# A two-layer graph network on one core: the activations' transposes move from TensorE to VectorE and DMA, with another order of tokens

## The chip, the core and the metric

The kernel runs on one core of one Trainium2 chip. The metric is the device time of one launch in microseconds, the median of several runs; smaller is better. Besides the timed runs there is one profiled execution, whose trace gives the start and length of each instruction on each engine. The engines are TensorE (PE, with its weight loads as PEld), VectorE (DVE), ScalarE (ACT), GpSimd (POOL) and SyncE (SP), which here issues every DMA.

## What is computed

The input `x` holds 64 graphs of 256 tokens with 512 features in float32, and `adj` is one 256 x 256 adjacency matrix for all of them. Each of two layers normalizes the tokens, applies a relu and adds its result to `x`:

```python
h = relu(layernorm(x));  x = x + (adj @ h) @ W0 + b0            # layer 0
h = relu(layernorm(x))                                          # layer 1, 8 heads of 64
q, k, v = h @ Wq + bq, h @ Wk + bk, h @ Wv + bv
s = q @ k.T / 8 + (1 - adj) * -1e9
x = x + (softmax(s) @ v) @ Wo + bo
```

All of it stays in float32. Layer 0 and the attention treat all tokens alike, so the tokens of a graph may be held in any order, as long as `adj` and the output are read and written in the same order.

## The kernel before

Two graphs make a group of 512 tokens, and 32 groups follow one another. In SBUF a tile has 128 partitions. `x` of a group is held by token, as four slices of 128 tokens with 512 features each (slices 0 and 1 are the first graph, k=0; slices 2 and 3 the second, k=1).

Five weight products (layer 0's `w`, then `q`, `k`, `v` and `o`) run through `project` (line 397), which computes a product of 2 x 2 blocks with seven block products in place of eight. For that GpSimd prepares sums of blocks of the activations, `t1` to `t4` (class `Halves`, lines 370 to 387), named `t_y`, `t_h` and `t_o` for the three inputs. One block product is 8 records on TensorE. In the order of `project` these are a11, a12, s2, s1, s3, a22, s4; the third (s2) is added on top of the first in the same PSUM bank, so it must wait until the first one's result has been read out, and it needs the sum t2.

The order of the work is written out by hand. The loop over groups (lines 706 to 726) puts these pieces after one another on TensorE: attention of group g, first half (`attend`, `pav` and `pden`); scores of its second half (`score`, line 608); output product of the group before (`post`, `o`); queries and keys of the next group (`queries_keys`); attention of the second half; scores of the next group; its values (`values`, `v`); and layer 0 of the group after next (`layer0`, `py` and `w`). Each engine works in program order. `after` and `tick` put work of the other engines a stated number of steps later. In each group TensorE needs 87 us for this round.

The step that changes stands at the start of `queries_keys`. The weight products want the activations with features on partitions. At the end of `layer0`, `finish` (line 500) adds and measures the result on VectorE, GpSimd computes the scales (`norm_scales`, lines 53 and 54), and ScalarE writes the normalized `h1` by token (line 512), k=0 first and then k=1. Later, `queries_keys` transposes `h1` into `h1T` with 16 TensorE transposes against an identity (line 525, tile `ph`, four PSUM banks), which ScalarE and VectorE copy out in turn (lines 527 and 529). GpSimd then forms `t_h` from `h1T` (line 387).

Three more places matter for the working. In `score`, VectorE reads each of eight score banks (line 613), and GpSimd subtracts the largest mask value (line 616). In `attend`, VectorE inverts the denominators in four pieces (line 656) and divides two tiles (line 660), which `post` uses as its input; GpSimd's `t_o` is formed directly behind the second division (lines 663 to 670). At the start, `adj` is transposed once on TensorE (line 318), and the masks are made from that copy (lines 328 to 339).

Eight PSUM banks are handed out in order by `bank` and `give`. `h1T` shares one buffer with layer 0's `yT` (tag "bT"), and the sums t1 to t4 rotate through eight buffers, two sets.

Of the kernel before, what the change touches and what calls it, by code (L numbers as in the profile page):

```python
# [13 lines left out]
P = 128  # L14
# [184 lines left out]
def kernel(  # L199
# [52 lines left out]
    def give(t):  # L252
        free_banks.append(bank_of.pop(id(t))[0])

    clock, later = [0], []

    def after(delay, fn, *args):
        later.append((clock[0] + delay, len(later), fn, args))  # L260

    def tick():
        clock[0] += 1
        due = sorted(e[:2] for e in later if e[0] <= clock[0])
        run_now = [e for d in due for e in later if e[:2] == d]
        later[:] = [e for e in later if e[0] > clock[0]]
        for _, _, fn, args in run_now:
            fn(*args)

    X, H0, Q, K, V, OT, HO = {}, {}, {}, {}, {}, {}, {}  # L270

    def load(g):
        X[g] = xpool.tile([P, T, D], F32, tag="x", name=f"x_{g}")
        src = x[g * GB:(g + 1) * GB].rearrange("b (t p) d -> p (b t) d", p=P)
        for t in range(0, T, 1 if g == 0 else T):
            e = t + (1 if g == 0 else T)
            nc.sync.dma_start(X[g][:, t:e, :], src[:, t:e, :])

    def quarter(xt, i, k):

# [1 line left out]


    load(0)
    adj_sb = tmp.tile([P, NT, N], F32, tag="u", name="adj_sb")
    nc.sync.dma_start(adj_sb, adj.rearrange("(t p) m -> p t m", p=P))
    w0_sb = load_weight(nc, const, w0, "w0_sb")
# [24 lines left out]


    adjT = const.tile([P, NT, N], F32, name="adjT")
    pa = bank([P, NT, N], "pa")
    for k in range(NT):
        for t in range(NT):
            nc.tensor.transpose(pa[:, k, t * P:(t + 1) * P], adj_sb[:, t, k * P:(k + 1) * P], ident)
    nc.vector.tensor_copy(adjT, pa)
    give(pa)  # L320

# [3 lines left out]
    top_b = top[:, None, :].to_broadcast([P, 2 * NT, N])  # L325

    def masks():
        nc.vector.tensor_scalar(maskT, adjT, -1.0, 1.0, op0=ALU.mult, op1=ALU.add)
        nc.vector.tensor_scalar(maskT, maskT, MASKED, None, op0=ALU.mult)
        nc.vector.tensor_scalar(adj_sb, adj_sb, -1.0, 1.0, op0=ALU.mult, op1=ALU.add)  # L330
        nc.vector.tensor_scalar(adj_sb, adj_sb, MASKED, None, op0=ALU.mult)
        rowmax = small.tile([P, NT], F32, tag="rowmax", name="rowmax", bufs=1)
        nc.vector.tensor_reduce(rowmax, adj_sb, AX.X, ALU.max)
        spread = tmp.tile([P, NT, P], F32, tag="u", name="spread")
        nc.vector.tensor_copy(spread, rowmax[:, :, None].to_broadcast([P, NT, P]))
        pt = bank([P, N], "pt")
        for t in range(NT):
            nc.tensor.transpose(pt[:, t * P:(t + 1) * P], spread[:, t, :], ident)
        nc.vector.tensor_copy(top, pt)
        give(pt)  # L340
# [15 lines left out]

    def weight_sums(eng, w, name):
        def part(i, j):  # L360
            return w[:, 2 * j:2 * j + 2, i * HF:(i + 1) * HF]
        s = {n: const.tile([P, 2, HF], F32, name=f"{name}_{n}") for n in ("s1", "s2", "s4")}
        eng.tensor_tensor(s["s1"], part(1, 0), part(1, 1), op=ALU.add)
        eng.tensor_tensor(s["s2"], s["s1"], part(0, 0), op=ALU.subtract)
        eng.tensor_tensor(part(1, 0), part(0, 0), part(1, 0), op=ALU.subtract)
        eng.tensor_tensor(s["s4"], part(0, 1), s["s2"], op=ALU.subtract)
        s.update(a11=part(0, 0), a12=part(0, 1), a22=part(1, 1), s3=part(1, 0))
        return s

    class Halves:  # L370

        def __init__(self, name, chunks):
            self.chunks = chunks
            self.t = {n: act.tile([P, 2, N], F32, tag="t", name=f"{n}_{name}", bufs=8)
                      for n in ("t1", "t2", "t3", "t4")}

        def b(self, j, k, c):
# [11 lines left out]
    def product(ps, s, a, halves, b, by_token, start=True, stop=True):  # L389
        for m in range(2):  # L390
            for c in range(2):
                w, y = s[a][:, c, :], halves.operand(b, c)
                lhs, rhs = (y, w) if by_token else (w, y)
                nc.tensor.matmul(ps[:, m, :], lhs[:, m * P:(m + 1) * P], rhs, start=(start and m + c == 0), stop=(c == 1),  # L394
                                 skip_group_check=True)

    def project(s, halves, by_token, name, read, finish, first_half_first=False):
# [67 lines left out]
        for t in range(T):  # L465
            after(start + T + 3 + t, relu, t)

    H1, H1T = {}, {}

    def layer0(g):  # L470

# [18 lines left out]

        mv = small.tile([P, T, 2], F32, tag="mv", name=f"mv1_{g}")
        st = [small.tile([P, 2, nc.vector.BN_STATS_DIM], F32, tag="st1", name=f"st1_{g}_{t}", bufs=8) for t in range(T)]
        h1 = H1[g] = act.tile([P, T, D], F32, tag="h", name=f"h1_{g}")
        done = []

        def read(ps, n):
# [15 lines left out]
                    nc.scalar.activation(h1[:, k * NT + t, :], xt[:, k * NT + t, :], AF.Relu,  # L512
                                         bias=nb[:, t:t + 1], scale=rs[:, t:t + 1])

        yield from project(W0, halves, True, f"w_{g}", read, finish)

    def queries_keys(g):

        xt, h1 = X[g], H1.pop(g)
        h1T = act.tile([P, DC, GN], F32, tag="bT", name=f"h1T_{g}")  # L520
        halves = H1T[g] = Halves(f"h_{g}", [h1T[:, d, :] for d in range(DC)])
        for t in range(T):
            ps = bank([P, DC, P], f"ph_{g}_{t}")
            for d in range(DC):
                nc.tensor.transpose(ps[:, d, :], h1[:, t, d * P:(d + 1) * P], ident)  # L525
            if t % 2:
                nc.vector.tensor_copy(h1T[:, :, t * P:(t + 1) * P], ps)  # L527
            else:
                nc.scalar.copy(h1T[:, :, t * P:(t + 1) * P], ps)
            give(ps)  # L530
        for c in range(2):
            halves.sums(nc.gpsimd, c, ("t1", "t2"))
        for c in range(2):
            halves.sums(nc.gpsimd, c, ("t3", "t4"))
        yield

        def out_bias_add(t):
            nc.gpsimd.tensor_tensor(xt[:, t, :], xt[:, t, :], bo_r, op=ALU.add)  # L538

        for s, bias, store, n in ((WQ, bq_c, Q, "q"), (WK, bk_c, K, "k")):  # L540
            store[g] = {}

            def read(ps, m):
                if m == 4:
                    return
                u = partial(f"{n}_{g}", m)
                for c in range(2):
                    f = 2 * (m == 3) + c
                    nc.scalar.activation(u[:, c, :], ps[:, c, :], AF.Identity, bias=bias[:, f:f + 1])
                return u  # L550

            def finish(ps, u, i, k):
                o = store[g][i, k] = act.tile([P, 2, N], F32, tag=f"{n}{i}{k}", name=f"{n}_{g}_{i}{k}")
                add(o, ps, u)

            if n == "k":
                for t in range(T):
                    after(2 * t + 1, out_bias_add, t)
            yield from project(s, halves, False, f"{n}_{g}", read, finish)

    def values(g):
        halves = H1T.pop(g)
# [10 lines left out]
            o = V[g][i, k] = act.tile([P, NT, HF], F32, tag=f"v{i}{k}", name=f"v_{g}_{i}{k}")  # L573
            add(o, ps, u)

        yield from project(WV, halves, True, f"v_{g}", read, finish)

    def post(g):

# [8 lines left out]
        def finish(ps, u, i, k):  # L588
# [1 line left out]
            add(o, ps, o)  # L590
            done.append(k)
            if done.count(k) == 2:
                nc.sync.dma_start(out[g * GB + k].rearrange("(t p) d -> p t d", p=P), xt[:, k * NT:(k + 1) * NT, :])

        yield from project(WO, halves, True, f"o_{g}", read, finish, first_half_first=g == NG - 1)

    A, AS = {}, {}

    def score(g, qd):


        for c in range(2):
            for b in range(GB):
# [11 lines left out]
                    give(ps[j])  # L615
                nc.gpsimd.tensor_tensor(a, a, top_b, op=ALU.subtract)  # L616
                after(3 + 2 * c + b, exponent, a)
                after(5 + 2 * c + b, key_sum, g, qd, c, b)

    def exponent(a):  # L620
        nc.scalar.activation(a, a, AF.Exp)  # L621
# [1 line left out]
    def key_sum(g, qd, c, b):  # L623
        s = AS[c, b] = att.tile([P, 2, N], F32, tag=f"as{c}{b}", name=f"as_{g}_{qd}_{c}{b}")
        a4 = A[c, b].rearrange("p (j k) n -> p j k n", j=2)
        nc.gpsimd.tensor_tensor(s, a4[:, :, 0, :], a4[:, :, 1, :], op=ALU.add)  # L626

    def attend(g, qd):

# [26 lines left out]
            nc.vector.reciprocal(rden[:, c * P:(c + 1) * P], den[:, c * P:(c + 1) * P])  # L656

        def divide():
            for f in range(2):
                nc.vector.tensor_tensor(o[f], po[f], rden, op=ALU.mult)  # L660
                give(po[f])
            nc.scalar.activation(den, rden, AF.Identity, accum_out=stats[:, 1, i:i + 1])
            if qd == (0 if g == NG - 1 else 1):
                HO[g] = Halves(f"o_{g}", chunks)
                for c in range(2):
                    HO[g].sums(nc.gpsimd, c, ("t1",))
            if qd == 1:
                for which in ("t2",), ("t3", "t4"):
                    for c in range(2):
                        HO[g].sums(nc.gpsimd, c, which)  # L670

        for c in range(4):
            after(1 + c, invert, c)
# [8 lines left out]
    load(1)  # L682
    for _ in range(T + 1):
        tick()
    W0 = weight_sums(nc.gpsimd, w0_sb, "w0")
    for _ in range(T + 2):
        tick()
    first = layer0(0)
    run(first, 1)
    masks()  # L690
    run(first, 3)
    WQ = weight_sums(nc.gpsimd, wq_sb, "wq")
    run(first)
    first = queries_keys(0)
    run(first, 1)
    WK = weight_sums(nc.gpsimd, wk_sb, "wk")
    run(first, 5)
    WV = weight_sums(nc.gpsimd, wv_sb, "wv")
    out_bias()
    ready(1, 0)  # L700
    run(first)
    WO = weight_sums(nc.gpsimd, wo_sb, "wo")
    score(0, 0)
    run(values(0))
    run(layer0(1))
    for g in range(NG):
        attend(g, 0)
        score(g, 1)
        tick()
        if g > 0:  # L710
# [64 lines left out]
```

## Time and profile before

| | us |
|---|---|
| median of 3 runs | 2841.37 (2840.2 to 2841.56) |
| profiled execution, its own time | 2842.41 |
| span of the profiled execution | 2840.6 |
| one steady round (start of `pav` of one group to that of the next) | 87.03 |
| TensorE transposes of `h1` (line 525): records, mean of one | 512, 276 ns |
| VectorE busy, share of the span | 52% |
| GpSimd busy, share of the span | 66% |
| DMA, share of 16 engines | 7.5% |

The profile has a page with six parts (busy time, slices of the span, DMA queues, the chain of work that ended last, groups of instructions, DMA issues), and the trace answers views such as a timeline of one engine in a window, the waits, or the busy time in stretches. A line of a timeline gives the start, the length, the engine, the line of the kernel, the operation, what is written and read, and the count of instructions merged; in brackets stands how long the engine had been idle and what ended that. Where instructions overlap at their ends, the distance between starts is the better measure of one.

### The profile page before, as it was taken

The page shows a single profiled execution, that of the slowest core. Times are in us where ns is not written, and L with a number is a line of the kernel's source. Part 1 is how long each engine was busy: PE and PEld are TensorE (multiplying, and loading weights), DVE is VectorE, ACT ScalarE, POOL GpSimd, SP SyncE. Part 2 cuts the span into 40 slices and gives each one's busy share as a digit, 9 for nine tenths or more (in the row PEclk, how much of TensorE's full clock was granted, in tenths as well). Part 3 has the DMA queues.
Part 4 walks back from the last instruction along what each step waited for, and adds up shares of the span by engine and source line. Part 5 has one row for each costly group of instructions (what it writes and reads, how often), then busy time and mean ns, then how long its engine had stood idle before and what let it go on. Part 6 is the DMA issues. An engine that isn't in the chain of part 4 may idle for free.

```text
span 2840.6 us, 43306 instructions
## 1 busy us (share of the span) xinstructions
PE 2799.5 (99%) x17680; PEld 2301.5 (81%) x17680; DVE 1478.2 (52%) x2703; ACT 851.7 (30%) x1441; POOL 1882.6 (66%) x1754
## 2 busy tenths in 40 slices
PE   6999999999999999999999999999999999999998
PEld 5788888888888888888888888888888888888886
DVE  3454545545555445455455554455554555545545
ACT  2332323323223233233232332332322323323221
POOL 5766666767567676676665676756766656767565
PEclk9999999999999999999999999999999999999999
DMA  4000000000000000000000000000000000000000
GB/s 130 1 1 30 31 31 30 1 30 31 31 31 21 11 30 31 30 31 1 30 31 31 30 16 16 30 31 31 30 1 30 31 31 31 10 22 30 31 16 31
DMA packets 39563, 75.97 MB, mean 27 GB/s; under 512 B 3520, under 2 KB 3776, under 8 KB 39360
## 3 DMA queue, kind: packets, MB, share of 16 engines
q1 hardware_dynamic: 39360, 73.15, 7.5%
q8 instruction: 141, 2.31, 0.3%
q14 instruction: 62, 0.51, 0.1%
HBM read 39.59 MB, written 33.55 MB: 26 GB/s over the span
## 4 chain that ended last, share of the span: by engine, by line
PE 96%; POOL 2%; DVE 1%; issue 1%; DMA 0%; ACT 0%; SPq 0%; DVEq 0%; POOLq 0%; ACTq 0%
PE sc L608 8%; PE py L480 8%; PE pav L638 8%; PE pden L644 2%; PE ph L525 2%; POOL a L616 1%; DVE x L441 0%; DVE a L613 0%; DMA adj_sb<-in_adj_dram 0%; PE q_0a L394 0%; PE o_25a L394 0%; PE o_17a L394 0%; PE o_5a L394 0%; PE o_7a L394 0%; PE o_4a L394 0%
## 5 line engine op out<-in xcount | busy, mean ns | idle before, releaser
L616 POOL TENSOR_TENSOR a<-a,top 128x1024 f32<-128x1024 f32 x256 | 597.1, 2368 | 189.0 <-DVE a L613 189.0
L53 POOL TENSOR_TENSOR rs<-rs,mhalf 128x2 f32<-128x2 f32 (+1 forms) x96 | 77.6, 809 | 553.9 <-DVE nb L52 553.9
L613 DVE SCALAR_TENSOR_TENSOR a<-sc,maskT 128x512 f32<-128x512 f32 x512 | 311.9, 681 | 230.1 <-PE sc L608 230.1
L626 POOL TENSOR_TENSOR as<-a 128x512 f32<-128x512 f32 x256 | 317.9, 1282 | 0.3 <-ACT a L621 0.3
L621 ACT ACTIVATE a<-a 128x1024 f32<-128x1024 f32 x256 | 266.7, 1054 | 136.6 <-POOL a L616 136.6
L608 PE MATMUL sc<-q,k 64*128 64x256 f32 x2048 | 250.1, 384 | 0.0
L608 PEld LDWEIGHTS sc<-q,k 64*128 64x128 f32 x2048 | 205.3, 186 | 45.5 <-PE pden L644 25.5
L480 PE MATMUL py<-adjT,h 128*128 128x256 f32 x1024 | 229.3, 382 | 6.7 <-ACT h L458 6.7
L512 ACT ACTIVATE h<-x,nb,rs 128x512 f32<-128x512 f32 x128 | 97.2, 806 | 460.6 <-POOL nb L54 460.6
L638 PE MATMUL pav<-a,v 128*32 128x256 f32 x4096 | 234.3, 381 | 0.0
L656 DVE RECIPROCAL rden<-den 128x128 f32<-128x128 f32 x256 | 231.8, 926 | 4.6 <-ACT den L652 4.6
L460 POOL TENSOR_TENSOR x<-x,b_r 128x512 f32<-128x512 f32 x128 | 162.5, 1282 | 103.2 <-ACT h L458 103.2
L480 PEld LDWEIGHTS py<-adjT,h 128*128 128x128 f32 x1024 | 196.4, 192 | 34.3 <-ACT h L458 7.4
L638 PEld LDWEIGHTS pav<-a,v 128*32 128x32 f32 x4096 | 126.5, 110 | 98.2 <-issue 21.2
L538 POOL TENSOR_TENSOR x<-x,bo_r 128x512 f32<-128x512 f32 x128 | 162.5, 1271 | 0.0
L482 ACT COPY yT<-py 128x512 f32<-128x512 f32 x128 | 75.0, 586 | 223.8 <-PE py L480 223.8
L387 POOL TENSOR_TENSOR t_h<-h1T 128x256 f32<-128x256 f32 x128 | 92.8, 725 | 72.8 <-DVE h1T L527 72.8
L458 ACT ACTIVATE h<-x,nb,rs 128x512 f32<-128x512 f32 x128 | 96.4, 806 | 11.0 <-POOL nb L54 11.0
L504 DVE BATCH_NORM_STATS2 st<-x 128x6 f32<-128x256 f32 x256 | 96.4, 419 | 4.4
L387 POOL TENSOR_TENSOR t_o<-oT,t_o 128x256 f32<-128x256 f32 x128 | 93.3, 743 | 7.8 <-DVE oT L660 7.8
L387 POOL TENSOR_TENSOR t_y<-yT,t_y 128x256 f32<-128x256 f32 x128 | 92.9, 726 | 5.8 <-ACT yT L482 0.8
L387 POOL TENSOR_TENSOR t_h<-h1T,t_h 128x256 f32<-128x256 f32 x128 | 92.8, 725 | 5.0
(2950 smaller groups left out, 5550.1 us busy)
## 6 DMA issues: line engine op xcount, KB each, us to landing
out_dram<-x SPq DMA_DIRECT2D x64, 512.0 KB, 2.8
x<-in_x_dram SPq DMA_DIRECT2D x31, 1024.0 KB, 5.4
x<-in_x_dram SPq DMA_DIRECT2D x4, 256.0 KB, 3.7
w_sb<-in_L_gnn_weight_dram SPq DMA_DIRECT2D x1, 1024.0 KB, 8.3
wq_sb<-in_L_gnn_Wq_dram SPq DMA_DIRECT2D x1, 1024.0 KB, 11.2
wk_sb<-in_L_gnn_Wk_dram SPq DMA_DIRECT2D x1, 1024.0 KB, 12.2
wv_sb<-in_L_gnn_Wv_dram SPq DMA_DIRECT2D x1, 1024.0 KB, 12.2
wo_sb<-in_L_gnn_Wo_dram SPq DMA_DIRECT2D x8, 128.0 KB, 4.6
```

The source lines that it names most:

```text
L387: eng.tensor_tensor(self.t[n][:, c, :], self.operand(p, c), self.operand(q, c), op=ALU.subtract)
L460: nc.gpsimd.tensor_tensor(xt[:, t, :], xt[:, t, :], b0_r, op=ALU.add)
L480: nc.tensor.matmul(ps[:, b * N:(b + 1) * N], h[:, b * NT + k, d * P:(d + 1) * P], adjT[:, k, :], start=(k == 0), stop=(k == NT - 1))
L512: nc.scalar.activation(h1[:, k * NT + t, :], xt[:, k * NT + t, :], AF.Relu, bias=nb[:, t:t + 1], scale=rs[:, t:t + 1])
L538: nc.gpsimd.tensor_tensor(xt[:, t, :], xt[:, t, :], bo_r, op=ALU.add)
L608: nc.tensor.matmul(ps[j][:, kt * N:(kt + 1) * N], k[j * HD:(j + 1) * HD, c, kt * P:(kt + 1) * P], q[j * HD:(j + 1) * HD, c, :], start=True ...
L613: nc.vector.scalar_tensor_tensor(a[:, j * NT:(j + 1) * NT, :].rearrange("p k n -> p (k n)"), ps[j], SCALE, maskT_f, op0=ALU.mult, op1=ALU.add)
L616: nc.gpsimd.tensor_tensor(a, a, top_b, op=ALU.subtract)
L621: nc.scalar.activation(a, a, AF.Exp)
L626: nc.gpsimd.tensor_tensor(s, a4[:, :, 0, :], a4[:, :, 1, :], op=ALU.add)
L638: nc.tensor.matmul(po[f][h * 32:(h + 1) * 32, b * N:(b + 1) * N], v[:, k, h * HD + f * 32:h * HD + f * 32 + 32], A[h // 2, b][:, (h % 2) * ...
L656: nc.vector.reciprocal(rden[:, c * P:(c + 1) * P], den[:, c * P:(c + 1) * P])
```

## The change

The transposes of `h1` leave TensorE. At the end of `layer0`, VectorE transposes each slice of `h1` in blocks of 32 x 32 into a new tile `r` (one instruction of 128 x 512 per slice, four per group). A block's 32 features then lie on the 32 partitions where the block's tokens had been, so DMAs carry the blocks to the partitions of their features: 16 DMAs for each graph, 32 for a group, each with 32 partitions, 4 chunks of features and 64 tokens (32 KB in pieces of 256 bytes). They are issued by SP. `queries_keys` starts at once with `t_h`.

So that the carried pieces are 64 tokens long, the tokens of a graph are ordered anew: a partition block i holds tokens 64 i to 64 i + 63, and slice t the half of them. `x` and the output are therefore moved in four DMAs per graph (before, one for a group in and one for a graph out), the division in `attend` writes its result in the new order with four instructions in place of two, and the copy of `adj` that layer 0 uses is loaded a second time by blocks and its columns are reordered by two VectorE copies ahead of the four transposes. The scores' mask stays in the old order, and since `adjT` no longer has that order, the mask is made from four more TensorE transposes inside `masks`.

To make room for `r`, the sums t1 to t4 have one set of buffers in place of two. Therefore `t_o` is no longer formed behind the division but at the start of the next round, after `attend(g, 0)` and ahead of `score(g, 1)`, and for the second half the pair sums (`key_sum`) come four steps later.

```diff
     def load(g):
         X[g] = xpool.tile([P, T, D], F32, tag="x", name=f"x_{g}")
-        src = x[g * GB:(g + 1) * GB].rearrange("b (t p) d -> p (b t) d", p=P)
-        for t in range(0, T, 1 if g == 0 else T):
-            e = t + (1 if g == 0 else T)
-            nc.sync.dma_start(X[g][:, t:e, :], src[:, t:e, :])
+        src = x[g * GB:(g + 1) * GB]
+        for k in range(GB):
+            for i in range(NI):
+                nc.sync.dma_start(X[g][32 * i:32 * i + 32, k * NT:(k + 1) * NT, :], by_block(src, i)[:, k])
...
+    adj_r = tmp.tile([P, NT, N], F32, tag="u", name="adj_r")
+    for i in range(NI):
+        nc.sync.dma_start(adj_r[32 * i:32 * i + 32], by_block(adj[None], i)[:, 0])
...
+    adj_p = tmp.tile([P, NT, N], F32, tag="u", name="adj_p")
+    for u in range(NT):
+        nc.vector.tensor_copy(adj_p[:, u, :].rearrange("p (t i b) -> p i t b", i=NI, t=NT),
+                              adj_r[:, u, :].rearrange("p (i t b) -> p i t b", i=NI, t=NT))
...
     def masks():
-        nc.vector.tensor_scalar(maskT, adjT, -1.0, 1.0, op0=ALU.mult, op1=ALU.add)
+        pm = bank([P, NT, N], "pm")
+        for k in range(NT):
+            for t in range(NT):
+                nc.tensor.transpose(pm[:, k, t * P:(t + 1) * P], adj_sb[:, t, k * P:(k + 1) * P], ident)
+        nc.vector.tensor_scalar(maskT, pm, -1.0, 1.0, op0=ALU.mult, op1=ALU.add)
...
-            self.t = {n: act.tile([P, 2, N], F32, tag="t", name=f"{n}_{name}", bufs=8)
+            self.t = {n: act.tile([P, 2, N], F32, tag="t", name=f"{n}_{name}", bufs=4)
...
+        h1T = H1T[g] = act.tile([P, DC, GN], F32, tag="bT", name=f"h1T_{g}")
+        for k in range(GB):
+            r = act.tile([P, DC * NI, NT, 32], F32, tag=f"r{k}", name=f"r_{g}_{k}")
+            for t in range(NT):
+                nc.vector.transpose(r[:, :, t, :], h1[:, k * NT + t, :].rearrange("p (j b) -> p j b", b=32))
+            blocks = r.rearrange("p (d j) t b -> p j d (t b)", j=NI)
+            for i in range(NI):
+                for j in range(NI):
+                    nc.sync.dma_start(h1T[32 * j:32 * j + 32, :, k * N + 64 * i:k * N + 64 * i + 64],
+                                      blocks[32 * i:32 * i + 32, j])
...
     def queries_keys(g):
-        for t in range(T):
-            ps = bank([P, DC, P], f"ph_{g}_{t}")
-            for d in range(DC):
-                nc.tensor.transpose(ps[:, d, :], h1[:, t, d * P:(d + 1) * P], ident)
-            if t % 2:
-                nc.vector.tensor_copy(h1T[:, :, t * P:(t + 1) * P], ps)
-            else:
-                nc.scalar.copy(h1T[:, :, t * P:(t + 1) * P], ps)
-            give(ps)
...
-                after(5 + 2 * c + b, key_sum, g, qd, c, b)
+                after((5 if qd == 0 else 9) + 2 * c + b, key_sum, g, qd, c, b)
...
+    def out_sums(g, which=("t1", "t2", "t3", "t4")):
+        if g not in HO:
+            HO[g] = Halves(f"o_{g}", OT[g])
+        for n in which:
+            for c in range(2):
+                HO[g].sums(nc.gpsimd, c, (n,))
...
             for f in range(2):
-                nc.vector.tensor_tensor(o[f], po[f], rden, op=ALU.mult)
+                for k in range(GB):
+                    src, den_k = (t[:, k * N:(k + 1) * N].rearrange("p (i t b) -> p i t b", i=NI, t=NT)
+                                  for t in (po[f], rden))
+                    dst = o[f][:, k * N:(k + 1) * N].rearrange("p (t i b) -> p i t b", i=NI, t=NT)
+                    nc.vector.tensor_tensor(dst, src, den_k, op=ALU.mult)
...
         attend(g, 0)
+        if g > 0:
+            out_sums(g - 1)
         score(g, 1)
```

The output is stored per graph in four DMAs of 32 partitions in the same order. The remaining lines of the diff (the counter of `after`, the dictionary `W`, a slice written in another place in `product`) leave the instructions as they are.

## The prediction

> **What bounds the kernel now.** The first view is the page: busy time, then the chain that ended last.
>
> ```profile
> span 2840.6 us, 43306 instructions
> PE 2799.5 (99%) x17680; PEld 2301.5 (81%) x17680; DVE 1478.2 (52%) x2703; ACT 851.7 (30%) x1441; POOL 1882.6 (66%) x1754
> ...
> PE 96%; POOL 2%; DVE 1%; issue 1%; DMA 0%; ACT 0%; SPq 0%; DVEq 0%; POOLq 0%; ACTq 0%
> PE sc L608 8%; PE py L480 8%; PE pav L638 8%; PE pden L644 2%; PE ph L525 2%; POOL a L616 1%; DVE x L441 0%; DVE a L613 0%; DMA adj_sb<-in_adj_dram 0%; PE q_0a L394 0%; PE o_25a L394 0%; PE o_17a L394 0%; PE o_5a L394 0%; PE o_7a L394 0%; PE o_4a L394 0%
> ```
>
> TensorE is the chain, and the transposes (ph) are 2% of it. So TensorE work taken away counts in full, unless another engine now makes TensorE wait. Hence the second view: one steady round, TensorE's timeline beside VectorE's and ScalarE's.
>
> ```profile
> 1591.98 3.66 PE L638 MATMUL pav<-a,v 128*32 128x256 f32 x64
> ...
> 1596.43 4.09 PE L608 MATMUL sc<-q,k 64*128 64x256 f32 x32
> ...
> 1604.01 1.98 PE L394 MATMUL o_16a<-wo_s,t_o 128*128 128x256 f32 x8
> ...
> 1612.79 1.91 PE L525 MATMUL ph<-ident,h 128*128 128x128 f32 x16
> 1614.77 1.97 PE L394 MATMUL q_18a<-h1T,wq_sb 128*128 128x256 f32 x8
> ```
>
> ```profile
> 1595.21 0.16 DVE L52 TENSOR_SCALAR nb<-mv 128x2 f32<-128x2 f32 x1
> 1597.67 4.87 DVE L613 SCALAR_TENSOR_TENSOR a<-sc,maskT 128x512 f32<-128x512 f32 x8 [2.29 <-PE sc L608]
> 1602.46 0.94 DVE L656 RECIPROCAL rden<-den 128x128 f32<-128x128 f32 x1
> 1603.32 0.62 DVE L441 TENSOR_TENSOR x<-o_16a,x 128x512 f32<-128x512 f32 x1
> ```
>
> ```profile
> 1594.50 1.52 ACT L512 ACTIVATE h<-x,nb,rs 128x512 f32<-128x512 f32 x2 [14.02 <-POOL nb L54]
> 1596.39 1.52 ACT L512 ACTIVATE h<-x,nb,rs 128x512 f32<-128x512 f32 x2 [0.37 <-POOL nb L54]
> ```
>
> The reader is to see two things, in rows that give start and length. From 1612.79 to 1614.77 the transposes hold TensorE 1.98 us. And VectorE has no slack at the start of a round: it reads eight score banks, inverts one piece and reads the product a11 (o_16a) until 1603.94; TensorE starts the product s2, which needs that read, at 1604.01. Slack: 0.07 us. VectorE's only rest before is 2.29 us, up to 1597.67, and there the new transposes go. I count from T0, the round's start (1591.98).
>
> **Steady rounds (30: transposes of groups 2 to 31).**
> Removed: 1.98 us each. The 16 banks' copies (0.69 on VectorE, 0.59 on ScalarE) lie beside TensorE; nothing.
>
> Added on VectorE: four transposes ahead of the score reads. The trace has no such instruction; the nearest rows are passes over 128 x 512, 4.87/8 = 0.61 us from start to start. Bounds 0.4 (a tensor_scalar over 512 at the start, L328, 0.42) and 1.4 (the broadcast copy L345, 1.44); I take 0.61, the row of equal size read once. They wait for ScalarE: the last slice of h1 is done at 1596.39 + 1.52 = 1597.91. So the last transpose ends at about 1597.95 + 0.61 = 1598.56, and the score reads start 0.89 late. Behind them queue the eight reads, the inversion and the read of a11, and for that TensorE waits: 0.89 - 0.07 = 0.82.
>
> By the Trainium skill (VectorE: DVE Perf Modes, The three transpose paths) a VectorE transpose of 128 x 128 takes 311 ns against TensorE's 390, and its rules give a 128 x 128 transpose to TensorE: this speaks against the change. No run here has its VectorE figure; the trace's transposes cost 1.98/16 = 0.124 us on TensorE, far below. With 4 x 0.311 = 1.24 us a slice as an estimate, the chain of four would end at 1600.4, the wait would be 2.6, and the whole would come to about 2899.
>
> Added on SP: 32 DMAs. Their price from the loads at the start:
>
> ```profile
> 25.06 0.42 SPq L302 DMA_DIRECT2D wo_sb<-in_L_gnn_Wo_dram  x1
> 25.53 0.42 SPq L303 DMA_DIRECT2D bv_c<-in_L_gnn_bv_dram  x1
> ```
>
> One each 0.47 us, for 128 KB as for 0.2 KB; landing 2.0 us (bv_c's row). The first can go when two slices are transposed, T0 + 4.85 (1596.75 plus a signal). The last lands at T0 + 4.85 + 31 x 0.47 + 2.0 = T0 + 21.4. GpSimd then needs 1.45 for t2's first half (two sums at 0.73), so T0 + 22.9. TensorE wants t2 in the third product of q: T0 + 12.03 + 0.82 + 8.78 (s2 to the end of o) + 3.53 (q's first two) = T0 + 25.2. So it arrives in time; it would not above (25.2 - 1.45 - 2.0 - 4.85)/31 = 0.55 us per DMA. For packets: the mean in the page's queue is 87 ns (7.5% of 16 engines' span over 39360), and in the window 25.6 to 26.1, where 77 of 93 are tiny, 21 ns (24.4% of 8 us over 93). Eight per engine and DMA give 0.17 to 0.69 us; I take the small end, so SP's issue rules. The moved x and output DMAs (8 and 8 a group at 0.47) have the rest of the round.
>
> Added on TensorE: h1T now comes from 32 DMAs on a few counters. At the start bv_c's issue waits for the landing of the DMA eight before it (SP's waits: L303 for wk_sb and for wv_sb), so there are eight counters, and q's first product has up to eight to look at. A second wait is an EVENT_SEMAPHORE of 51 ns in TensorE's queue (the view of line 394 counts 171); seven make 0.36, and the later product that reads k=1 may do it again. I take 0.45, bounds 0 and 0.75.
>
> GpSimd's t_o sums (8 x 0.69 = 5.5 us) move to T0 + 4.4 to 9.9, ahead of the subtraction, which starts 3 us later and ends near T0 + 19.3; t_h waits for T0 + 21.4 anyway. The subtraction's delay reaches ScalarE's exponentials and the second attention only at T0 + 47. Nothing. The division in four pieces: VectorE has 0.56 idle behind it, which covers some 0.2.
>
> Sum: -1.98 + 0.82 + 0.45 = -0.71 us a round, -21.3 for 30.
>
> **The start, where nothing covers the DMAs.**
>
> ```profile
> 47.17 0.72 POOL L387 TENSOR_TENSOR t_h<-h1T 128x256 f32<-128x256 f32 x1 [3.75 <-DVE h1T L527]
> ...
> 132.92 0.73 POOL L387 TENSOR_TENSOR t_h<-h1T 128x256 f32<-128x256 f32 x1
> ```
>
> Group 0: layer 0 ends on TensorE at 38.92 (its last product's start, 37.19, and 1.73); t_h began 8.25 us later and sets the third product of q (49.71). Now 21.4: +13.2. Group 1 has no output product to cover it (T0 = 116.61): t_h began at T0 + 16.3, now 21.4: +5.1. Masks: their chain on VectorE (14.14 to 17.26) lay under the first relu; now it waits for four transposes behind the first py (1.09, the row of pa), then takes 3.12 + 0.19, all before the transposes of spread (L338): +4.4. The adj copies: two at about 0.4 ahead of adjT: +0.8 (0 to 3). TensorE after a gap of 2 us runs slowly for a while: v_0c took 3.55 in place of 1.73 behind 1.99 idle; I add 1.8 once (0 to 7). Sum +25.3. Lower bound 17: with 0.38 per DMA, a lone x load's issue, the last lands at T0 + 18.6, so 10.4 + 2.3 + 4.4 are left. Upper bound 38: with 0.55 it lands at T0 + 23.9, so 15.6 + 7.6 + 4.4, with 3 and 7 for the others.
>
> The end: waits of pden for GpSimd's pair sums (1.15 + 0.59) go, since t_o no longer stands before them; three more output DMAs, 1.4. -0.3.
>
> **Total.** -21.3 + 25.3 - 0.3 = +3.7 on the profiled execution's 2842.41, which is 1.04 above the median of the runs: 2845 for the median. The gain is spent at the start.
>
> **Rivals.**
> Faster: TensorE's looks at the counters cost nothing and the start its lower bound: 30 x (-1.98 + 0.82) = -34.8, + 17: 2823. For it: TensorE's queue runs ahead of the array. Against: products with a second wait start their successor after 1.83 instead of 1.73, so waits do show.
>
> Slower: transposed data late. Place: the third product of q in each round. From 0.55 us per DMA. At 0.6 t2 comes at T0 + 26.9, 1.4 to 1.7 late: 30 x (-0.71 + 1.5) = +24, and the start 25 + 8 (4 later in either group): 2898. At 0.69 (packets of 87 ns) about 2988. Transposes at their bound of 1.4 would make VectorE's reads 3.3 late: 30 x (-1.98 + 3.3 + 0.45) + 25 = +78, 2919. Against: SP's even 0.47, and 21 ns for small packets.
>
> That the change does not do what it says: the 512 records leave for certain; only the masks keep four more, priced above.
>
> **How the numbers follow.** Even, 0.50: 2845, own range 2832 to 2858. Faster, 0.25: 2823 (2812 to 2832). Slower, 0.25: 2898 (2860 to 2990). A measurement tells 0.2% (5.7 us) from no change. Faster by more: 0.25 + 0.06 of the even case = 0.31. Within: 0.25. Slower: 0.25 + 0.19 = 0.44. The range leaves out 0.02 below and the upper 0.12 of the slower case: 2815 to 2895.
>
> **What would show it.** Steady round near 86.3 instead of 87.03; score reads at T0 + 6.6 instead of 5.69, behind four transposes of 0.6; s2 of o waiting for VectorE by 0.8; 32 DMAs in 15 us, the last landed at T0 + 21; t_h of group 0 some 21 us after layer 0's end; a gap of 4 us before L338's transposes. Wrong if the transposes take over 1 us, if the DMAs' distance is not 0.47, or if q waits for t_h in steady rounds.

## The result, and the profile after

The kernel became slower: 3072.08 us (median of 4 runs, 3066.39 to 3073.91) against 2841.47 in the same session, a ratio of 1.0809 with a 95% interval of 1.0791 to 1.0828. The forecast was 2845, its range ended at 2895; the sign was the one to which the prediction had given the largest chance, the size was far outside.

The page of the kernel after: span, busy time, the chain that ended last (its first lines), one group of section 5 and one line of the DMA issues.

```profile
span 3071.6 us, 44749 instructions
PE 2847.8 (93%) x17172; PEld 2301.4 (75%) x17172; DVE 1536.7 (50%) x2897; ACT 818.1 (27%) x1377; POOL 1880.6 (61%) x1754
...
PE 71%; SPq 11%; DVE 9%; POOL 3%; issue 3%; DMA 2%; POOLq 0%; ACT 0%; DVEq 0%; ACTq 0%
...
L409 POOL TENSOR_TENSOR t_h<-h1T 128x256 f32<-128x256 f32 x128 | 92.5, 723 | 302.3 <-DMA h1T<-r 274.2
...
h1T<-r SPq DMA_DIRECT2D x1024, 32.0 KB, 1.9
```

TensorE was 96% of the chain and is now 71%; SP's queue, which was 0%, is 11%. So a ninth of the chain that sets the end passes in an engine that computes nothing. The group line says where it enters: GpSimd's t_h stood idle 274.2 us for the carried h1T, about 9 us in each round. PE's busy time rose by 48 us although 508 records went: a sign of slow products, to which we come below.

One steady round of the kernel after, TensorE's timeline (start, length; in brackets the idle time before and what ended it):

```profile
1637.50 3.66 PE L669 MATMUL pav<-a,v 128*32 128x256 f32 x64
...
1641.96 4.58 PE L632 MATMUL sc<-q,k 64*128 64x256 f32 x32
...
1650.49 1.97 PE L416 MATMUL o_15a<-wo_s,t_o 128*128 128x256 f32 x8 [0.31 <-DVE x L463]
...
1659.25 1.89 PE L416 MATMUL q_17a<-h1T,wq_sb 128*128 128x256 f32 x8
1660.97 1.89 PE L416 MATMUL q_17b<-h1T,wq_sb 128*128 128x256 f32 x8
1667.25 0.77 PE L416 MATMUL q_17a<-t_h,wq_s 128*128 128x256 f32 x2 [4.39 <-POOL t_h L409]
1668.73 2.93 PE L416 MATMUL q_17a<-t_h,wq_s 128*128 128x256 f32 x6 [0.71 <-POOL t_h L409]
1671.45 3.44 PE L416 MATMUL q_17c<-t_h,wq_s 128*128 128x256 f32 x8
1674.73 1.89 PE L416 MATMUL q_17a<-t_h,wq_sb 128*128 128x256 f32 x8
```

The same round on the other engines: VectorE, SP's queue and GpSimd.

```profile
1640.87 1.42 DVE L543 STREAM_TRANSPOSE r<-h 128x512 f32<-128x512 f32 x2
1642.76 1.42 DVE L543 STREAM_TRANSPOSE r<-h 128x512 f32<-128x512 f32 x2 [0.47 <-ACT h L534]
1644.10 1.25 DVE L637 SCALAR_TENSOR_TENSOR a<-sc,maskT 128x512 f32<-128x512 f32 x2
```

```profile
1642.43 21.50 SPq L547 DMA_DIRECT2D h1T<-r  x32
1664.03 3.91 SPq L616 DMA_DIRECT2D out_dram<-x  x8
```

```profile
1647.32 9.33 POOL L640 TENSOR_TENSOR a<-a,top 128x1024 f32<-128x1024 f32 x4
1665.68 0.72 POOL L409 TENSOR_TENSOR t_h<-h1T 128x256 f32<-128x256 f32 x1 [9.03 <-DMA h1T<-r]
```

Read from T0 = 1637.50. SP's first carrying DMA goes at T0 + 4.93, as predicted (4.85). But 32 of them take 21.50 us, 0.67 each and not 0.47. So t_h starts at T0 + 28.2 instead of 21.4, and q's third product, which could have started at 1662.70, waits. Two more things are to be seen in TensorE's rows. First, after the wait the products are slow: q_17c takes 3.44 where such a product takes 1.89. Second, from q_17b's start 13.76 us pass to the start of the fifth product, where three products of 1.73 would make 5.2: this round lost 8.57 us there. (It took 94.4 us, one of the longer ones; the steady rounds of this kernel lie between 92.5 and 94.8.)

The windows view of the same kernel (window, then busy time and count of each engine, the granted TensorE clock, the DMA share and GB/s) gives the clock of the slow stretch and of an earlier one:

```profile
1666.50:1675.00 8.50, 7.04 (x18) 5.35 (x19) 0.00 (x0) 0.84 (x2) 8.42 (x10) 0.60 0.73 199
1646.00:1660.00 14.00, 13.69 (x64) 11.39 (x62) 12.54 (x21) 4.84 (x6) 10.65 (x6) 1.00 0.21 48
```

The granted clock was 0.60 on average in the 8.5 us behind the wait, and 1.00 before. The second row has another use: in the stretch in which SP issues the carrying DMAs, the DMA engines are only 21% busy. They are not the limit; the issuing is.

### The profile page after: what moved, and what is told of

Same layout as the page of the kernel before. It is cut to its first block, busy times and chain, and to the rows that moved or that the text cites. A ratio compares the mean times of both kernels' runs of the same rounds, so it can differ in the third digit from the quotient of the medians.

```text
span 3071.6 us, 44749 instructions
## 1 busy us (share of the span) xinstructions
PE 2847.8 (93%) x17172; PEld 2301.4 (75%) x17172; DVE 1536.7 (50%) x2897; ACT 818.1 (27%) x1377; POOL 1880.6 (61%) x1754
## 2 busy tenths in 40 slices
DMA packets 193961, 109.97 MB, mean 36 GB/s; under 512 B 157648, under 2 KB 158160, under 8 KB 193744
## 3 DMA queue, kind: packets, MB, share of 16 engines
q1 hardware_dynamic: 193744, 107.06, 13.8%
## 4 chain that ended last, share of the span: by engine, by line
PE 71%; SPq 11%; DVE 9%; POOL 3%; issue 3%; DMA 2%; POOLq 0%; ACT 0%; DVEq 0%; ACTq 0%
SPq L547 11%; PE py L502 7%; PE pav L669 7%; PE sc L632 6%; DVE a L637 4%; POOL t_h L409 3%; DMA h1T<-r 2%; DVE x L463 2%; DVE rden L687 2%; PE pden L675 2%; DVE st L526 0%; POOLq L409 0%; PE v_29a L416 0%; PE v_26a L416 0%; PE v_23a L416 0%
## 5 line engine op out<-in xcount | busy, mean ns | idle before, releaser
L409 POOL TENSOR_TENSOR t_h<-h1T 128x256 f32<-128x256 f32 x128 | 92.5, 723 | 302.3 <-DMA h1T<-r 274.2
L632 PE MATMUL sc<-q,k 64*128 64x256 f32 x2048 | 265.1, 389 | 0.0
L632 PEld LDWEIGHTS sc<-q,k 64*128 64x128 f32 x2048 | 208.9, 186 | 56.7 <-PE pden L675 13.2
L409 POOL TENSOR_TENSOR t_y<-yT 128x256 f32<-128x256 f32 x128 | 93.2, 728 | 31.2 <-ACT yT L504 31.2
L543 DVE STREAM_TRANSPOSE r<-h 128x512 f32<-128x512 f32 x128 | 90.5, 711 | 15.1 <-ACT h L534 15.1
```

Source lines behind the costliest of these rows:

```text
L409: eng.tensor_tensor(self.t[n][:, c, :], self.operand(p, c), self.operand(q, c), op=ALU.subtract)
L632: nc.tensor.matmul(ps[j][:, kt * N:(kt + 1) * N], k[j * HD:(j + 1) * HD, c, kt * P:(kt + 1) * P], q[j * HD:(j + 1) * HD, c, :], start=True ...
```

## The experiments

The kernels are named here and explained below. The table gives, beside the times, three parts of each profiled execution: the time to the first attention of group 1, the mean of the 29 rounds from there to the first attention of group 30, and what is left.

| kernel | median us | ratio to before, interval | start | mean round | rest |
|---|---|---|---|---|---|
| before | 2839.76, 2840.35 | | 199.25 | 87.05 | 117.0 |
| after | 3072.08 | 1.0809, 1.0791 to 1.0828 | 234.88 | 93.56 | 123.5 |
| warm | 3002.14 | 1.0574, 1.0557 to 1.0592 | 232.89 | 91.24 | 120.7 |
| pe_back | 2843.52 | 1.0015, 1.0005 to 1.0024 | 198.34 | 87.09 | 116.9 |
| dve_alone | 2872.19 | 1.0110, 1.0093 to 1.0127 | 202.00 | 87.97 | 118.7 |
| split | 2828.24 | 0.9959, 0.9945 to 0.9973 | 222.72 | 85.85 | 116.0 |
| wide | 2826.55 | 0.9953, 0.9937 to 0.9970 | 218.16 | 85.84 | 115.7 |
| best | 2800.17 | 0.9859, 0.9842 to 0.9875 | 192.37 | 85.84 | 115.7 |

The first median of before was taken beside warm, pe_back and split, the second beside dve_alone, wide and best. The 231.0 us that the span grew are 35.6 at the start, 29 x 6.51 = 188.8 in the rounds, and 6.5 in the rest, which holds one more such round.

The theory after the result: SP pays more for a DMA from SBUF to SBUF than for the loads from HBM that gave the predicted price; most of the rest follows from the late data. The rivals: the price comes from the four pieces of 256 bytes per partition; or from bytes and counters; and, for the size of the loss, VectorE's transposes.

### issue_cost: what one DMA costs its issuer

A kernel by itself that computes nothing of the reference: stages of 24 equal DMAs, one stage after the other has landed, differing in source, pieces and issuer.

```python
for m in range(24):
    nc.sync.dma_start(z[0:32, m % 8], a[32:64])          # 4 pieces of 256 bytes per partition, from SBUF
...
    nc.sync.dma_start(z[0:32, m % 8], x[0:4, 0:32, 0:64].rearrange("s p e -> p s e"))   # the same from HBM
...
    (nc.scalar if m % 2 else nc.sync).dma_start(z[0:32, m % 8], a[32:64])
```

> This kernel computes nothing of the reference: it only issues 24 DMAs each of twelve shapes, 32 partitions unless named, one shape after the other with VectorE reading the result between them. Disputed: why SP took 0.66 us for each carrying DMA (0.60 busy) where the loads with 64 pieces of 2 KB took 0.47. Theory A, pieces: the price of an issue grows with the number of pieces per partition and hardly with their size: 1 piece 0.35 to 0.45, 2 pieces 0.45, 4 pieces 0.6 to 0.66, 8 pieces 0.9 to 1.1; 4 pieces of 64 floats, of 128 floats and of 16 floats within 0.05 of each other; the same from HBM. Theory B, source: a read from SBUF is what costs; then all SBUF shapes lie near 0.66, 2x2048 from SBUF too, and 4x256 from HBM near 0.47. Theory C, the DMA engines or the eight counters hold SP back: then the issues come in bursts, idle times of SP stand before them, and the price follows the bytes (4x512 dearer than 4x256). Issued half by ScalarE: if the two queues issue independently, the 24 take half the time of the SP stage (about 8 us instead of 16); if they share what is short, the same 16.

SP's queue in that kernel. The name of a tile gives the pieces; L49 and L69 have 4 pieces of 256 and 512 bytes, L64 one of 256, L59 eight of 256, L74 two of 2048; L84 and L89 read HBM, L104 moves all 128 partitions.

```profile
1.49 15.59 SPq L49 DMA_DIRECT2D z_4x<-a_4x  x24
...
36.71 15.97 SPq L59 DMA_DIRECT2D z_8x<-a_8x  x24
54.54 15.12 SPq L64 DMA_DIRECT2D z_1x<-a_1x  x24
72.12 15.47 SPq L69 DMA_DIRECT2D z_4x<-a_4x  x24
91.39 15.34 SPq L74 DMA_DIRECT2D z_2x<-a_2x  x24
...
124.26 11.81 SPq L84 DMA_DIRECT2D z_dram4x<-in_x_dram  x24
136.12 12.90 SPq L89 DMA_DIRECT2D z_dram2x<-in_x_dram  x24
171.89 7.70 SPq L99 DMA_DIRECT2D z_both4x<-a_both4x  x12
182.05 16.58 SPq L104 DMA_DIRECT2D z_all4x<-a_all4x  x24
```

One piece or eight, 256 bytes or 2048: 15.1 to 16.0 us for 24, that is 0.63 to 0.67 us each. What matters here is the source: the same four pieces of 256 bytes take 11.81, 0.49 each, when they come from HBM, and two of 2048 take 0.54 (in these 12.90 us SP waited 3.0 for landings). That is near the price of the prediction's rows, and those rows were loads from HBM. All these DMAs write to SBUF, and a row above shows that reading SBUF is not dear by itself: the kernel after stores its output from SBUF to HBM, and SP issues eight of these DMAs in 3.91 us, 0.49 each (out_dram). So the dear DMA is the one with both ends in SBUF. A DMA over 128 partitions, with four times the bytes, costs 0.69. The rival of the pieces falls, and that of the bytes too. Why two ends in SBUF cost more is not shown. And L99: twelve on SP and twelve on ScalarE side by side take 7.7 us, so the two issue independently.

### warm: how much of the loss is the clock

Ten products that nobody reads (20 records) are put between q's second and third, where TensorE waits, for groups 2 to 31.

```diff
+        if name[:2] == "q_" and int(name[2:]) >= 2:
+            pw = bank([P, 2, N], f"{name}warm")
+            for n in range(FILL):
+                nc.tensor.matmul(pw[:, n % 2, :], ident, maskT[:, n % 2, :], start=True, stop=True)
+            give(pw)
         product(pa, s, "s2", halves, "t2", by_token, start=False, stop=False)
```

> The changed kernel with ten products that nobody reads (20 records, 4.3 us) put on TensorE in each round from group 2 on, where it waits for the third product of q. Theory: the round's loss at that place (7.0 to 8.6 us from the end of the second to the start of the fifth product, beyond their own length) is only 4 to 5 us of waiting for late data; the rest, about 3 us, is TensorE running at about half speed after the wait. Then the added work makes the kernel faster: about 30 x 3 = 90 us, to 2980. Rival: the slow products wait for something else (GpSimd's sums, a bank); then the time stays at 3072, or grows if the added work overshoots the wait.

```profile
1626.10 4.48 PE L441 MATMUL q_17warm<-maskT,ident 128*128 128x256 f32 x20
1630.41 0.62 PE L418 MATMUL q_17a<-t_h,wq_s 128*128 128x256 f32 x2
1631.82 1.56 PE L418 MATMUL q_17a<-t_h,wq_s 128*128 128x256 f32 x6 [0.78 <-POOL t_h L411]
1633.22 1.89 PE L418 MATMUL q_17c<-t_h,wq_s 128*128 128x256 f32 x8
```

The windows view for the same stretch (columns as above):

```profile
1630.00:1640.00 10.00, 9.22 (x42) 7.44 (x41) 2.06 (x4) 1.68 (x4) 9.92 (x12) 1.00 0.65 166
```

The wait is filled with work of no use, and the kernel is 70 us faster, which is 30 times the difference of the rounds, 93.56 - 91.24 = 2.32. That is less than the 90 us expected. Behind the filler q_17c takes 1.89 again, and the granted clock is 1.00. So of the 7.72 us by which a round of the kernel after exceeds one without late data (85.84, kernel wide), 2.3 are the clock's and 5.4 the waiting's. The row of 0.60 agrees with the rule of the Trainium skill (TensorE: Matmul & The Clock Gate, section "Why this matters for your kernels") that idle gaps of TensorE over some 3 us between bursts are to be avoided; the gap here was 4.4 us. But 3 us is no safe bound in this case: in the kernel before, the product v_0c took 3.55 us behind a gap of 1.99 us (its row stands under best).

### pe_back and dve_alone: the parts that are not the carrying

pe_back puts the TensorE transposes back into `queries_keys` and leaves out VectorE's transposes and the 32 DMAs; the new order of tokens, the masks and all moves stay. dve_alone is pe_back with VectorE's transposes added, into a tile that nobody reads.

```diff
-        xt, h1T = X[g], H1T[g]
+        xt = X[g]
+        h1 = H1.pop(g)
+        h1T = act.tile([P, DC, GN], F32, tag="bT", name=f"h1T_{g}")
+        for t in range(T):
+            ps = bank([P, DC, P], f"ph_{g}_{t}")
+            for d in range(DC):
+                nc.tensor.transpose(ps[:, d, :], h1[:, t, d * P:(d + 1) * P], ident)
...
```

> The changed kernel with the transposes of h1 back on TensorE in queries_keys (copied out in the new order of tokens), no transposes on VectorE and no carrying DMAs; the new token order, loads, stores, masks, divided division and moved sums stay. Theory: all of the loss in steady rounds belongs to the carrying DMAs and VectorE's transposes, so a steady round is 87.0 within 0.2 us and only the masks at the start remain: about 9 us, 2850 to 2856. Rival: a third or more of the 230 us belongs to the moved sums, the small x DMAs or the division; then 2900 or more.

> The TensorE transposes are back and feed queries_keys, and VectorE does its 32x32 transposes too, into a tile that nobody reads; no carrying DMA. Theory (VectorE's four transposes hold up the readings of the scores by 0.93 us a round, as the round after shows): 2843.5 of the kernel with TensorE's transposes alone + 31 rounds of 0.93 = about 2872, with 1 transpose group on VectorE of 2.8 us ahead of L613's readings in the trace. Rival (the lateness is made up within the round, since TensorE's next wait ends on another engine): within 5 us of 2843.5.

pe_back has the round of the kernel before (87.09 against 87.05) and nearly its start: the masks lose 6.7 us there up to layer 0's first product (33.48 in place of 26.82), and later places give this back, the product v_0c 3.8 of it (see best). Everything outside the transposition costs 4 us together, where about 9 were expected. With VectorE's transposes the round grows to 87.97 and the time to 2872, as expected. The cause is to be seen in dve_alone on TensorE, and then on VectorE:

```profile
1614.12 4.58 PE L641 MATMUL sc<-q,k 64*128 64x256 f32 x32
...
1622.65 1.97 PE L416 MATMUL o_16a<-wo_s,t_o 128*128 128x256 f32 x8 [0.31 <-DVE x L463]
```

```profile
1614.92 1.42 DVE L543 STREAM_TRANSPOSE r<-h 128x512 f32<-128x512 f32 x2 [0.47 <-ACT h L534]
1616.26 4.84 DVE L646 SCALAR_TENSOR_TENSOR a<-sc,maskT 128x512 f32<-128x512 f32 x8
```

The reads of the scores start at T0 + 6.60 behind the transposes (T0 is 1609.66 in this run), the scores take 4.58 instead of 4.09, and s2 waits for VectorE: the same rows as in the kernel after. So VectorE's part is 0.9 us a round, and its place is the one that the prediction named.

### split and wide: the same data, issued sooner

split leaves 22 of the 32 DMAs on SP and lets ScalarE issue the last ten behind its reading of the denominators. wide stays on SP alone and carries both graphs of a group together: 16 DMAs of eight pieces, with the same bytes in pieces of the same size.

```diff
+                    d = (h1T[32 * j:32 * j + 32, :, k * N + 64 * i:k * N + 64 * i + 64], blocks[32 * i:32 * i + 32, j])
+                    if k * NI * NI + i * NI + j < ON_SP:
+                        nc.sync.dma_start(*d)
+                    else:
+                        REST.append(d)
```

```diff
+        r = act.tile([P, DC, GB, NI, NT, 32], F32, tag="r", name=f"r_{g}")
...
+        blocks = r.rearrange("p d k j t b -> p j (d k) (t b)")
+        for i in range(NI):
+            for j in range(NI):
+                dst = h1T[32 * j:32 * j + 32].rearrange("p d (k n) -> p (d k) n", k=GB)
+                nc.sync.dma_start(dst[:, :, 64 * i:64 * i + 64], blocks[32 * i:32 * i + 32, j])
```

> The changed kernel with 22 of the 32 carrying DMAs on SP and the last ten issued by ScalarE behind its reading of the denominators. Theory: the loss is SP's serial issue; if the two queues issue side by side, the last lands near T0 + 21.4 instead of 27.9, q's third product does not wait, and a steady round is 87.03 - 2.0 (transposes) + 0.93 (VectorE's score reads late) = 86.0; with some 28 us lost at the start 2835 to 2845. Rival: both queues share what is short, the carrying takes as long as before, 3060 to 3080. Third way: ScalarE is late with the exponentials because of ten issues of 0.6 us; then TensorE waits at the attention instead, and the round lies between.

> The kernel after the change with the two graphs of a group carried together: 16 DMAs a group instead of 32, each with eight pieces of 256 bytes per partition instead of four, all on SP; the bytes and the number of packets are the same. Theory (SP pays by the DMA, 0.65 us, whatever is in it): 16 x 0.65 = 10.4 us; the first starts when all four transposes are done, T0 + 6.7, the last lands by T0 + 19.2, ahead of T0 + 25.2; q's third product does not wait, the round is 85.8 us as with the divided issue, and the start is about 10 us shorter than there (16 issues fewer in group 0): 2815 to 2828. Rival (the time goes by bytes, packets or pieces): 21 us of carrying as in the changed kernel, 3060 to 3075.

wide, SP's queue, and TensorE's rows where the wait had been:

```profile
1598.46 10.85 SPq L548 DMA_DIRECT2D h1T<-r  x16
```

```profile
1613.39 1.89 PE L416 MATMUL q_18a<-h1T,wq_sb 128*128 128x256 f32 x8
1615.12 1.89 PE L416 MATMUL q_18b<-h1T,wq_sb 128*128 128x256 f32 x8
1616.85 1.89 PE L416 MATMUL q_18a<-t_h,wq_s 128*128 128x256 f32 x8
```

Half the DMAs take half the time, 0.68 each, and the wait is gone; split, with its 14.44 us on SP and 6.51 on ScalarE, ends in the same round, 85.85. Both are faster than the kernel before, by 0.4 to 0.5%, and split is better than its forecast of 2835 to 2845. So it is the time of issuing, and neither bytes nor packets, that made the data late: wide moves the same bytes as the kernel after (107.03 against 107.06 MB) in only 4% fewer packets (185552 against 193744). One expectation on wide failed: its start is 4.6 us shorter than split's, not 10. In group 0 a DMA of wide needs the transposes of both graphs, and q's first product waited 19.45 us for it (17.06 in the kernel after). The Trainium skill says (DMA: Bandwidth & Descriptors, section "Issuing engines are not separate DMA queues") that issuing from several engines only saves the sequencer's time to initiate, "which is usually small relative to the DMA itself". The first half agrees with split. The second does not hold here: one DMA's 0.67 us of issuing is a third of its 1.9 us to landing, and as the issues follow one another, 32 of them take 21.5 us while the DMA engines are 21% busy.

### best: the start repaired as well

wide, but groups 0 and 1 are transposed by TensorE, and the four transposes of the mask go ahead, right behind those of `adj`, so that VectorE's chain for the row maxima lies under other work again.

```diff
+    pm = bank([P, NT, N], "pm")
+    for k in range(NT):
+        for t in range(NT):
+            nc.tensor.transpose(pm[:, k, t * P:(t + 1) * P], adj_sb[:, t, k * P:(k + 1) * P], ident)
+    nc.vector.tensor_scalar(maskT, pm, -1.0, 1.0, op0=ALU.mult, op1=ALU.add)
+    give(pm)
+
     def masks():
...
+        if g < 2:
+            H1[g] = h1
+            return
```

> As the kernel with 16 DMAs, but groups 0 and 1, which have no attention beside them, are transposed by TensorE as in the kernel before, and the mask's transposes are issued right behind the adjacency's, so that the transposition of the row maxima does not wait for VectorE. Theory (all of the loss that is left is at the start: 23.5 us to the attention of group 2 with the divided issue): the start within 4 us of the kernel before, 30 rounds 1.2 us shorter each: 2840 - 36 + 4 = 2808, at least 15 us under the kernel before. Rival (the rounds' gain is given back where VectorE changes over, or the start's loss lies in the adjacency's new order and not in the carrying): 2820 or more.

2800.17 us, 1.4% below the kernel before and 8 us better than expected. The rounds give 29 x 1.21 = 35 us. The start is 6.9 us shorter than before, not up to 4 longer. The largest part is at the product v_0c, which in the kernel before waited 1.99 us and then ran slowly, and does not wait in this one. The kernel before:

```profile
93.98 3.55 PE L394 MATMUL v_0c<-wv_s,h1T 128*128 128x256 f32 x8 [1.99 <-POOL a L616]
97.32 7.22 PE L480 MATMUL py<-adjT,h 128*128 128x256 f32 x32
```

The kernel best:

```profile
90.75 1.89 PE L417 MATMUL v_0c<-wv_s,h1T 128*128 128x256 f32 x8
92.48 7.07 PE L503 MATMUL py<-adjT,h 128*128 128x256 f32 x32
```

From the first scores (76.63) to the last row 15.85 us pass; in the kernel before it was 97.32 - 77.71 = 19.61, so 3.8 us are won here. Of the other 3.1, 1.1 lie before the first scores and 1.9 between the first attentions of groups 0 and 1 (80.76 against 82.64). pe_back also has 15.85 at v_0c, so it belongs to those parts of the change that pe_back keeps, not to the transposition. Which of them did it was not tried.

## Why the prediction was wrong, step by step

**The step that failed: SP's price.** "One each 0.47 us, for 128 KB as for 0.2 KB" was read from two loads of HBM and carried over to DMAs from SBUF to SBUF. That the size does not matter was right (issue_cost: 256 bytes or 2048, the same). That the two ends do not matter was assumed without a row, and they do: 0.49 with one end in HBM (loads, and the output's stores from SBUF too), 0.63 to 0.67 with both in SBUF. The threshold of 0.55 stands between the two, so by the prediction's own sum some 0.15 us per issue decided whether the data come in time. With 0.67 in the prediction's own sum the last DMA lands at T0 + 4.9 + 31 x 0.67 + 1.9 = T0 + 27.6, and t_h began at T0 + 28.2. The trace of before held no DMA from SBUF to SBUF; the price was an unknown, and its upper bound should have reached the "slower" rival at full weight. The rival's mechanism and place were right, and its threshold fits these prices. Its size fell short: at 0.69 it had 2988, at the measured 0.67 there are 3072.

**What the rival's price left out: the clock, and the second half of t2.** The clock is 2.3 us a round, 70 us in all (warm). The prediction had seen in the start's rows that TensorE runs slowly after a gap, and charged it once, not in each round that waits. It also counted with the first half of t2 alone. GpSimd makes the second half 1.48 us later, and the third product's second part waits for it: it starts 1.48 us behind the first (1668.73 and 1667.25), where a quarter of a product is 0.43. That is 1.05 us more in each round.

**VectorE's transposes: right.** Predicted 0.61 from start to start, and 0.82 us a round; measured 0.67 (1.34 from the third one's start to the score reads), and 0.9 (dve_alone). The score reads started at T0 + 6.60, as predicted. The skill's figure, weighed in the prediction as 1.24 a slice, is given there for bf16; it is not what this trace shows for its 128 x 512 slice in float32: 0.711 long.

**The transposes removed: right.** dve_alone to wide, 87.97 to 85.84, is 2.1 us, where -1.98 was the term.

**TensorE's look at the counters: wrong, 0 and not 0.45.** In the steady rounds q's first product starts 1.78 behind o's last, as the transposes did in the kernel before, and its second 1.72 behind the first, without a gap. So a round whose data come in time changes by -1.21 (wide), better than the predicted -0.71.

**The start: +35.6, predicted +25.3.** Masks: layer 0's product starts at 35.59 in place of 26.82, +8.8, predicted 4.4 and 0.8 for the copies of adj, which cost 0.1 (the first py starts at 16.88 in place of 16.78). The wait for the row maxima alone was 6.1: three passes of VectorE's chain took 1.37 to 1.48 each, in place of 0.42 in the kernel before, while GpSimd was adding to x; whether that slowed them was not tried. The 24 py records behind the wait took 7.65 in place of 6.21. Group 0: from there to q's third product 41.63 in place of 22.89, +18.7, predicted 13.2; group 1: +10.2 between the attentions of groups 0 and 1, predicted 5.1. Both fit 0.67 per DMA and the slow products behind each gap. v_0c gave 3.8 back, which was not foreseen, and 1.7 are lost between these places.

**The division in four pieces, GpSimd's moved sums and the other DMAs: nothing in the rounds, as predicted.** pe_back holds them all and has the round of before.

## What to carry to other kernels

Price a DMA from a row with the same kind of source and destination, and where none is in the trace, let the bound reach past the threshold that decides. When many small transfers replace one engine's work, count their issues before their bytes: fewer and wider ones, or a second issuer, turned a loss of 8% into a small gain here (0.4 to 0.5%). A wait of TensorE can cost more than its length, since the products behind it may run at a lower clock (5.4 us of waiting and 2.3 of clock in a round here); and where nothing covers the new path (the first groups), keep the old one.

## What the runs showed of the hardware that was not expected

- Issuing a DMA on SP took 0.63 to 0.67 us from SBUF to SBUF (32 partitions, one to eight pieces, 256 bytes to 4 KB per partition), 0.49 to 0.54 from HBM to SBUF, and 0.49 from SBUF to HBM. On ScalarE it was 0.65 from SBUF to SBUF (6.51 us for ten).
- SP and ScalarE issued side by side without slowing each other: twelve each in 7.7 to 8.1 us.
- Behind a gap of 4.4 us TensorE's granted clock was 0.60 over 8.5 us; with the gap filled it was 1.00, and the product q_17c took 1.89 us in place of 3.44. Behind a gap of 1.99 us a product took 3.55.
- A VectorE transposition of 128 x 512 in float32 took 0.711 us, against 0.69 for an addition of that size.
